# A delta rule's products: VectorE in program order too, copies ahead of SiLUs, sums two chunks at a time, first tiles normed ahead of the weights

## The chip, the cores and the metric

The kernel runs on one core of a Trainium2 chip. The metric is the device time of one execution, in microseconds (us). A core has the engines TensorE (PE; its weight loads are shown apart, as PEld), VectorE (DVE), ScalarE (ACT) and GpSimd (POOL), and SyncE (SP), which here only issues DMAs. Each engine takes its instructions in the order of its own list, and an instruction at the head of a list that waits for another engine holds up all that stand behind it.

## The reference

The kernel computes one block on x, 128 sequences of T = 32 tokens, so 4096 tokens of width 512, in f32: a cross attention, a gated delta rule with its MLP, and a feed-forward part with ternary weights. The part that matters here, with 32 heads of width 16:

```python
h = _rms(x, attn_norm_w)                       # x is layer-normed first
q = silu(silu(_causal_dwconv(h @ Wq.T, conv_q)))   # 4 taps along a sequence
k = silu(silu(_causal_dwconv(h @ Wk.T, conv_k)))
v = silu(silu(_causal_dwconv(h @ Wv.T, conv_v)))
q, k = _l2norm(q by heads), _l2norm(k by heads)
beta = sigmoid(h @ Wbeta.T)
def step(S, (kt, qt, vt, bt)):
    err = S kt - vt
    S = S - bt * outer(err, kt)
    return S, S qt
```

The kernel does not step through the tokens. For each sequence and head it forms the products of all k with all k and all q (32 x 32 each); the k-k products give a triangular system, which is solved by forward substitution for all sequences and heads of a group at once; the q-k products, masked, and the k then give the outputs.

## The kernel before

The program has four stages, one after the other, with some work of a later stage beside an earlier one: the cross attention (0 to about 687 us in the profile), `delta_products` (702 to 1223), `delta_out_mlp` (outputs, MLP and the rest of the substitution, to 2366) and the ternary feed-forward part (to the end). The change lies in the second.

`delta_products` takes the tokens in 8 groups of 512 (NG, SG; GT = 4 tiles of 128 tokens). A group is one round, `a_round`, or `last_round` for the last. A round has 12 steps, one for each 128 channels of k, q and v: k0, q0, k1, q1, ..., then v0 to v3 (the last round goes through k, v, q). Each step does this:

- `channels` (L614): four matmuls of 128x512 into a PSUM tile pp (three buffers); ScalarE copies it into acc, scaled by the last tap (three buffers); VectorE adds the three other taps, each reading and writing acc (L625).
- `activated` (L634): two SiLUs on ScalarE, on the acc of the step before. After a step of q, `masked` calls `hold` (L646), which spreads kq by heads into a zeroed operand kqm (three buffers) with eight DMAs on SP (`masked_operand`, L511).
- `multiply` (L653), in eight of the twelve steps (`due`): `products` (L519), 32 small matmuls pg<-kqm,kq into two PSUM tiles, two ScalarE copies kk<-pg, and on GpSimd the store of the k-k half, the mask and the store of the q-k half.
- `Group.square` and `Group.add`: squares of k and q on ScalarE, and their sums by heads on TensorE, into three column groups of 32 rows of one PSUM tile pn, the middle one being the logits of beta.
- In steps 7 to 10, `normed` (L605): a tile of the next group is normed on VectorE (hn, two buffers), turned by four TensorE transposes and copied to hT by ScalarE.
- `behind_round`, for the group before: `by_tokens` turns lengths and beta to rows of tokens, `put_q` and `put_v` store them and the scaled v, `inverted` inverts the lengths of q (rl).

Beside the rounds from the second on, `mixed` (L106) takes steps of `Substitution.solve` (L471) between the steps of the round, in proportion: `SHARE` units of cost a round, where one solve has 82 units and 8 for the landing of its loads. Its work is on VectorE: for each token s, a scaling of W by a column (L493), a product pr of L with the solved row (L497) and a subtraction from all the rows behind (L503), so the operations get shorter from 128x1984 down to 128x64. Its loads (L in four pieces, W in one) go through SP.

TensorE and ScalarE take the instructions of this stage in program order: `InOrder` (L141) chains each instruction to the one before, and so their rows in the profile all carry L151. VectorE, GpSimd and SP are ordered by a planner, which follows the engines' estimated times and the buffers. Before the first round, `scaled_rows` (L453) multiplies the weights wk, wq, wv and wb by the norm's weights, on VectorE, in 16 slices, and four GpSimd memsets (L1476) clear um and pe, two operands that the third stage uses.

## Time and profile before

| what | value |
|---|---|
| median of three runs | 2940.22 us (2938.33 to 2943.78) |
| the profiled execution's own time | 2938.77 us |
| its span, first to last instruction | 2937.0 us |
| TensorE busy | 2823.2 us, 96% |
| VectorE busy | 1995.4 us, 68% |
| ScalarE busy | 1033.0 us, 35% |
| GpSimd busy | 682.5 us, 23% |
| mean granted clock of TensorE | 0.988 |

In rows of the profile, L12 is line 12 of the kernel. A row of a group names the line, the engine, the operation, output <- inputs by the program's names, and the shape (partitions x elements). A wait is put down to the instruction whose end released it. In a time line, a row has start and duration, and in brackets how long the engine was idle before it, and the releaser; consecutive alike instructions share a row (xN), and their duration is that of the whole row.

### The profile page before, as it was taken

Reading aid. Unit: us, or ns where it says so; the run is one execution under the profiler, and the core shown is the slowest. Engines: PE = TensorE matmul, PEld = TensorE weight load, DVE = VectorE, ACT = ScalarE, POOL = GpSimd, SP = SyncE. Lnnn points to the kernel's source line nnn. Section 1 sums busy time; section 2 is a strip of 40 time slices with the busy share of each in tenths; the row PEclk is TensorE's granted clock in tenths of the full one; section 3 lists DMA queues with packets and bytes.
Section 4 is the critical chain, followed back from the end, with each engine's and each line's share of the span. In section 5 each row is a group of like instructions: output and inputs, shape, how many; then the busy total and the mean of one; then the engine's idle time right before and its main releaser. Section 6 shows DMA issues by size and latency. Waiting matters only on the chain.

```text
span 2937.0 us, 42773 instructions
## 1 busy us (share of the span) xinstructions
PE 2823.2 (96%) x15895; PEld 1658.6 (56%) x15958; DVE 1995.4 (68%) x3317; ACT 1033.0 (35%) x1766; POOL 682.5 (23%) x974
## 2 busy tenths in 40 slices
PE   8999999997999899999999999999999989999997
PEld 3434343443443344566676767777777756666664
DVE  3353544325599995678787878888722289999996
ACT  1111111213666466521122212112211146776774
POOL 1121212212777677321212111101000000000000
PEclk9999999999999999999999999999999999999999
DMA  9898998874555545841414141313231124434433
GB/s 316 275 306 295 337 315 278 280 243 123 149 165 155 163 141 145 242 140 56 130 54 132 56 130 52 122 57 98 71 108 33 35 74 90 87 81 88 89 71 69
DMA packets 342815, 429.64 MB, mean 146 GB/s; under 512 B 149712, under 2 KB 250192, under 8 KB 340176
## 3 DMA queue, kind: packets, MB, share of 16 engines
q1 hardware_dynamic: 305696, 324.36, 37.0%
q0 software_dynamic: 36912, 102.55, 11.7%
q8 instruction: 127, 2.08, 0.3%
q14 instruction: 80, 0.66, 0.1%
HBM read 288.88 MB, written 94.37 MB: 130 GB/s over the span
## 4 chain that ended last, share of the span: by engine, by line
PE 59%; DVE 10%; issue 2%; DMA 2%; POOL 1%; ACT 1%; SPq 1%; ACTq 0%; DVEq 0%; POOLq 0%
PE ps L151 18%; PE pm L1009 9%; PE pm L1020 9%; PE pm L1012 9%; PE pp L151 5%; PE ps L983 4%; DVE W L503 2%; DVE pr L497 2%; DVE acc L625 2%; PE ps L953 2%; PE pg L151 1%; PE pn L151 1%; DMA xs<-x 1%; POOL kk L541 1%; DVE m L151 1%
## 5 line engine op out<-in xcount | busy, mean ns | idle before, releaser
L1009 PE MATMUL pm<-hT,wg 128*128 128x256 f32 x1408 | 343.1, 386 | 0.2 <-ACT hT L998 0.2
L1012 PE MATMUL pm<-hT,wu 128*128 128x256 f32 x1408 | 336.8, 382 | 1.3 <-DVE wu L1070 1.3
L497 DVE TENSOR_TENSOR pr<-L,W 128x1984 f32<-128x1984 f32 (+30 forms) x248 | 307.3, 1239 | 9.1 <-DMA L<-ld 4.6
L503 DVE TENSOR_TENSOR W<-W,pr 128x1984 f32<-128x1984 f32 (+30 forms) x248 | 309.7, 1249 | 2.8
L1020 PE MATMUL pm<-wd,mT 128*128 128x512 f32 x704 | 307.4, 592 | 0.0
L1009 PEld LDWEIGHTS pm<-hT,wg 128*128 128x128 f32 x1408 | 263.9, 191 | 51.0 <-issue 11.5
L1012 PEld LDWEIGHTS pm<-hT,wu 128*128 128x128 f32 x1408 | 268.7, 191 | 38.7 <-DVE wu L1070 1.6
L1020 PEld LDWEIGHTS pm<-wd,mT 128*128 128x128 f32 x704 | 132.4, 190 | 160.2 <-issue 160.2
L151 PE MATMUL ps<-wq,qT 128*128 128x512 bf16 x930 | 215.5, 379 | 6.2 <-ACT t L151 4.6
L1014 ACT ACTIVATE sg<-pm 128x256 f32<-128x256 f32 x176 | 67.4, 383 | 331.4 <-PE pm L1009 319.7
L1015 DVE TENSOR_TENSOR mT<-pm,sg 128x256 f32<-128x256 f32 x176 | 74.0, 420 | 158.7 <-PE pm L1012 155.0
L151 PEld LDWEIGHTS <-qT 128*128 128x128 bf16 x960 | 94.0, 98 | 105.3 <-issue 5.5
L151 DVE TENSOR_TENSOR mb<-m 128x1024 f32<-128x1024 f32 x128 | 153.2, 1217 | 0.1
L151 DVE TENSOR_TENSOR m<-mb 128x1024 f32<-128x1024 f32 x128 | 150.8, 1219 | 1.2
L1343 POOL DMA_DIRECT2D xo<-x x31 | 26.4, 851 | 526.4 <-ACT xo L151 492.0
L151 ACT ACTIVATE t<-ps,magic,qs 128x512 f32<-128x512 f32 x158 | 115.7, 781 | 39.5 <-DVE qs L151 39.4
L537 POOL DMA_DIRECT2D ld<-kk x128 | 93.6, 731 | 147.6 <-ACT kk L151 120.5
L541 POOL TENSOR_TENSOR kk<-kk,cm 128x256 f32<-128x256 f32 x128 | 126.3, 987 | 2.7
L151 PEld LDWEIGHTS ps<-hd,mT 128*128 128x128 f32 x1024 | 119.1, 192 | 8.9 <-ACT mT L151 4.8
L151 PE MATMUL ps<-hd,mT 128*128 128x128 f32 x1024 | 119.8, 275 | 4.0 <-ACT mT L151 4.0
L151 PE MATMUL ps<-wq,q2T 128*128 128x512 bf16 x481 | 116.2, 384 | 5.4 <-DMA q2T<-q 3.7
L151 PE MATMUL pp<-hT,wk 128*128 128x512 f32 x256 | 120.3, 614 | 0.7 <-ACT hT L151 0.7
(224 smaller groups left out, 4751.2 us busy)
## 6 DMA issues: line engine op xcount, KB each, us to landing
kall<-in_ctxT_dram SPq DMA_DIRECT2D x32, 2056.0 KB
cx<-in_ctx_dram SPq DMA_DIRECT2D x32, 2048.0 KB
x<-xo POOLq DMA_DIRECT2D x64, 256.0 KB, 3.5
ld<-kk POOLq DMA_DIRECT2D x128, 128.0 KB, 2.6
pd<-kk POOLq DMA_DIRECT2D x128, 128.0 KB, 2.6
L<-ld SPq DMA_DIRECT2D x32, 512.0 KB
pe<-pd SPq DMA_DIRECT2D x256, 64.0 KB
kqm<-kq SPq DMA_DIRECT2D x448, 32.0 KB
```

The lines of the kernel that those rows point to most:

```text
L151: got = method(*args, **kw)
L497: nc.vector.tensor_mul(pr[:, 0:n], bc(L[:, s, :, s + 1 : T].rearrange("p h t -> p t h"), HD), w[:, s].unsqueeze(1).to_broadcast([P, n, H4, ...
L503: nc.vector.tensor_sub(w[:, s + 1 :], w[:, s + 1 :], pr[:, 0:n])
L537: nc.gpsimd.dma_start(ld[r].rearrange("(i p) f -> p i f", p=P), kk[:, 0].rearrange("p i h t -> p i (h t)"))
L541: nc.gpsimd.tensor_mul(q, q, cm.unsqueeze(1).to_broadcast([P, 2 * H4, T]))
L625: last = nc.vector.scalar_tensor_tensor(acc[:, :, d:], pp[:, :, : T - d], cw[n][:, ec, TAPS - 1 - d : TAPS - d], acc[:, :, d:], ALU.mult, ...
L983: nc.tensor.matmul(pw, oT[:, i, dc, :], wo[:, dc, :], start=dc == 0, stop=dc == DC - 1)
L1009: nc.tensor.matmul(pg, wg[:, dc, fs], hT[:, dc, :], start=dc == 0, stop=dc == DC - 1)
L1012: nc.tensor.matmul(pu, wu[:, dc, fs], hT[:, dc, :], start=dc == 0, stop=dc == DC - 1)
L1014: nc.scalar.activation(sg, pg, AF.Silu)
L1015: mark[:] = [nc.vector.tensor_mul(mT[:, fc, :], pu, sg).ins]
L1020: nc.tensor.matmul(pd, mT[:, fc, i * P : (i + 1) * P], wd[:, fc, :], start=fc == 0, stop=fc == FC - 1,)
```

## The change

VectorE gets an `InOrder` as well, for the products and for the parts of the substitution that run beside them, so it takes its instructions as the program writes them: the three taps of a step one behind the other, then the round's other work, then the pieces of the substitution. In each step `multiply` comes ahead of `activated`. The sums of squares are made for two chunks of channels at once, into four column groups, at two steps of a round instead of four; beta's logits are made apart, at the end of a round, with a transpose of their own; lengths and beta are taken to tokens accordingly. At the start, the first four tiles are normed and turned ahead of the scaling of the weights, and wq is scaled on ScalarE. The norm of a tile (`normed`) now comes one step ahead of its transposes (`turned`). The clearing of um and pe is done by twelve VectorE memsets in the first round, four to a step. The substitution's loads on SP are chained behind the last kqm transfer (`Substitution.load`, `queue`).

```diff
...
 PACE = 45.0
-def scaled_rows(nc, wp, name, norm, ws, engine=None):
-    mul = engine.mul if engine else nc.vector.tensor_scalar_mul
-    nw = wp.tile([P, DC], FP, name=name, bufs=1)
-    nc.sync.dma_start(nw, norm.rearrange("(c p) -> p c", p=P))
-    for t in ws:
-        for dc in range(DC):
-            mul(t[:, dc, :], t[:, dc, :], nw[:, dc : dc + 1])
+def scaled_rows(mul, t, nw):
+    for dc in range(DC):
+        mul(t[:, dc, :], t[:, dc, :], nw[:, dc : dc + 1])
 class Substitution:
...
     def __init__(self, g, pool, ld, vd, ud):
-        self.nc, self.pool, self.ld, self.vd, self.ud = g.nc, pool, ld, vd, ud
+        self.tc, self.nc, self.pool = g.tc, g.nc, pool
+        self.ld, self.vd, self.ud = ld, vd, ud
+        self.dve, self.queue = g.nc.vector, {}
+    def load(self, dst, src):
+        got = self.nc.sync.dma_start(dst, src)
+        if "last" in self.queue:
+            follow(self.tc, got.ins, self.queue["last"])
+            self.queue["last"] = got.ins
     def solve(self, gi):
...
-            nc.vector.tensor_mul(w[:, s], w[:, s], bc(W[:, s, :, HD], HD))
+            self.dve.tensor_mul(w[:, s], w[:, s], bc(W[:, s, :, HD], HD))
...
-                nc.vector.tensor_sub(w[:, s + 1 :], w[:, s + 1 :], pr[:, 0:n])
+                self.dve.tensor_sub(w[:, s + 1 :], w[:, s + 1 :], pr[:, 0:n])
...
     for h in range(HH):
         rows = slice(h * HD, (h + 1) * HD)
-        nc.sync.dma_start(m[rows, h % H4], kq[rows])
+        last = nc.sync.dma_start(m[rows, h % H4], kq[rows])
+    return last.ins
 def products(nc, pe, act, banks, pool, ld, pd, k, m, cm):
...
         )
     )
     pe = InOrder(tc, nc.tensor)
     act = InOrder(tc, nc.scalar)
+    dve = substitution.dve = InOrder(tc, nc.vector)
+    queue = substitution.queue
     with stack:
         w, cw = {}, {}
         for n, src, p in (("k", wkT, wp1), ("v", wvT, wp1), ("q", wqT, wp1)):
...
         nc.sync.dma_start(hs, heads.rearrange("(c p) h -> p c h", p=P))
         cm = wp.tile([P, T], FP, name="cm")
         nc.sync.dma_start(cm, causal)
-        scaled_rows(nc, wp, "nw", norm_w, [w["k"], w["q"], w["v"], w["b"]])
+        nw = wp.tile([P, DC], FP, name="nw")
+        nc.sync.dma_start(nw, norm_w.rearrange("(c p) -> p c", p=P))
         kqm = [wp3.tile([P, H4, 2, KT], FP, name=f"kqm{i}") for i in range(3)]
-        blank = [t[:, h] for t in kqm for h in range(H4)]
+        blank = [t[:, h] for t in kqm for h in range(H4)] + blanks
         mv, rs = stats
         def load(n):
...
             nc.sync.dma_start(xt, x1[n * P : (n + 1) * P, :])
             return xt
-        def normed(n, xt, hT):
+        def normed(n, xt):
+            hn = hp.tile([P, D], FP, name="hn")
+            dve.tensor_scalar(hn, xt, mv[:, n, 0:1], rs[:, n, 1:2], ALU.subtract, ALU.mult)
+            return hn
+        def turned(n, hn, hT):
             i = n % GT
-            hn = hp.tile([P, D], FP, name="hn")
-            nc.vector.tensor_scalar(
-                hn, xt, mv[:, n, 0:1], rs[:, n, 1:2], ALU.subtract, ALU.mult
-            )
             act.copy(hT[:, :, i * P : (i + 1) * P], g.transposed(ps, hn, g.ident, pe=pe))
         def channels(hT, n, ec):
...
             acc = wk.tile([P, GB, T], FP, name="acc", bufs=3)
             act.activation(acc, pp, AF.Copy, scale=cw[n][:, ec, TAPS - 1 : TAPS])
             for d in range(1, TAPS):
-                last = nc.vector.scalar_tensor_tensor(
+                dve.scalar_tensor_tensor(
                     acc[:, :, d:], pp[:, :, : T - d], cw[n][:, ec, TAPS - 1 - d : TAPS - d],
                     acc[:, :, d:], ALU.mult, ALU.add,
                 )
-            return acc.rearrange("p b t -> p (b t)"), last.ins
+            return acc.rearrange("p b t -> p (b t)")
         waiting = []
...
             while len(held) < min(len(pieces), count["done"] + len(kqm)):
                 gi, ec, half, kq = pieces[len(held)]
                 m = kqm[len(held) % len(kqm)]
-                masked_operand(nc, m, kq[:, :, half * KT : (half + 1) * KT])
+                queue["last"] = masked_operand(nc, m, kq[:, :, half * KT : (half + 1) * KT])
                 held.append(m)
         def multiply():
...
             def __init__(self, gi):
                 self.gi = gi
-                self.sums = psn.tile([3 * H, SG], FP, name="pn")
-                self.v = {}
+                self.v, self.sq = {}, []
             def square(self, kq, of="kq"):
                 sq = wk.tile([P, 2, SG], FP, name="sq")
                 ns = slice("kq".index(of[0]), "kq".index(of[-1]) + 1)
                 act.activation(sq[:, ns], kq[:, ns], AF.Square)
-                return sq
-            def add(self, sq, hT, ec, of="kq"):
-                at = dict(start=ec == 0, stop=ec == DC - 1)
+                self.sq.append(sq)
+            def add(self, ec, of="kq"):
+                if ec == 0 and "k" in of:
+                    self.sums = psn.tile([4 * H, SG], FP, name="pn")
+                for n in of:
+                    for r in range(2):
+                        at = (2 * "kq".index(n) + r) * H
+                        last = pe.matmul(
+                            self.sums[at : at + H], hs[:, ec + r, :], self.sq[r][:, "kq".index(n)],
+                            start=ec == 0, stop=ec == DC - 2,
+                        )
+                self.sq.clear()
+                return last
+            def logits(self, hT):
+                pb = ps.tile([P, P], FP, name="ps")
+                for dc in range(DC):
+                    for i in range(GT):
+                        pe.matmul(
+                            pb[i * H : (i + 1) * H], w["b"][:, dc, :], hT[:, dc, i * P : (i + 1) * P],
+                            start=dc == 0, stop=dc == DC - 1,
+                        )
+                self.tanh = st.tile([P, P], FP, name="tanh")
+                act.activation(self.tanh, pb, AF.Tanh, scale=0.5)
+            def lengths(self, of="kq"):
                 if "k" in of:
-                    pe.matmul(self.sums[0:H], hs[:, ec, :], sq[:, 0], **at)
-                    pe.matmul(
-                        self.sums[H : 2 * H], w["b"][:, ec, :], hT[:, ec, :], **at
-                    )
-                if "q" in of:
-                    return pe.matmul(self.sums[2 * H :], hs[:, ec, :], sq[:, 1], **at)
-            def lengths(self, of="kq"):
-                if "k" in of:
-                    f = self.factors = wk.tile([3 * H, SG], FP, name="f", bufs=1)
-                    act.activation(f[H : 2 * H], self.sums[H : 2 * H], AF.Tanh, scale=0.5)
-                for n, r in (("k", slice(0, H)), ("q", slice(2 * H, 3 * H))):
-                    if n in of:
-                        act.activation(self.factors[r], self.sums[r], AF.Sqrt)
+                    self.factors = wk.tile([4 * H, SG], FP, name="f", bufs=1)
+                r = slice("kq".index(of[0]) * 2 * H, ("kq".index(of[-1]) + 1) * 2 * H)
+                act.activation(self.factors[r], self.sums[r], AF.Sqrt)
             def by_tokens(self):
                 f = self.factors
-                pt = ps.tile([P, GT, 2 * H], FP, name="ps")
+                pt = ps.tile([P, GT + 2, 2, H], FP, name="ps")
                 for i in range(GT):
                     pe.transpose(
-                        pt[:, i, :], f[0 : 2 * H, i * P : (i + 1) * P], g.ident[0 : 2 * H, 0 : 2 * H]
+                        pt[:, i].rearrange("p r h -> p (r h)"), f[0 : 2 * H, i * P : (i + 1) * P],
+                        g.ident[0 : 2 * H, 0 : 2 * H],
                     )
+                pe.transpose(pt[:, GT:].rearrange("p i r h -> p (i r h)"), self.tanh, g.ident)
                 self.n = st.tile([P, GT, H], FP, name="n")
-                nc.vector.tensor_scalar_max(self.n, pt[:, :, 0:H], 1e-12)
+                for r in range(2):
+                    to, of = (
+                        t.rearrange("p i (c r h) -> p i c r h", c=2, r=2)[:, :, :, r]
+                        for t in (self.n, pt[:, 0:GT, r])
+                    )
+                    dve.tensor_scalar_max(to, of, 1e-12)
                 self.beta = st.tile([P, GT, H], FP, name="beta")
-                nc.vector.tensor_scalar(self.beta, pt[:, :, H:], 0.5, 0.5, ALU.mult, ALU.add)
+                dve.tensor_scalar(
+                    self.beta.rearrange("p i h -> p (i h)"),
+                    pt[:, GT:].rearrange("p i r h -> p (i r h)"), 0.5, 0.5, ALU.mult, ALU.add,
+                )
                 n2 = st.tile([P, GT, H], FP, name="n2", bufs=1)
...
             def put_q(self):
                 for c in range(DC):
-                    rows = slice(2 * H + c * HH, 2 * H + (c + 1) * HH)
+                    at = (2 + c % 2) * H + c * HH
+                    rows = slice(at, at + HH)
...
-                nc.vector.tensor_mul(
+                dve.tensor_mul(
                     vt[:, :, :, 0:HD], pv.rearrange("p i (h v) -> p i h v", v=HD),
                     bc(self.n[:, :, h], HD),
                 )
...
-                acc, last = channels(hT, n, ec)
-                with tc.issue_after(last):
-                    for _ in range(min(H4, len(blank))):
-                        nc.vector.memset(blank.pop(0), 0.0)
+                acc = channels(hT, n, ec)
+                for _ in range(min(H4, len(blank))):
+                    dve.memset(blank.pop(0), 0.0)
+                if due[j] and count["done"] < len(held) and (old or j >= 4):
+                    multiply()
                 activated()
                 waiting.append((acc, dst, masked(ec) if n == "q" else kept))
-                if due[j] and count["done"] < len(held) and (old or j >= 4):
-                    multiply()
                 if 3 <= j <= 9 and j % 2:
-                    sq = new.square(kq[(j - 3) // 2])
-                if 4 <= j <= 10 and j % 2 == 0:
-                    new.add(sq, hT, (j - 4) // 2)
+                    new.square(kq[(j - 3) // 2])
+                if j in (6, 10):
+                    new.add((j - 6) // 2)
                 if j in loads:
                     xt.append(load((gi + 1) * GT + len(xt)))
                 if j == 9 and gi == 0:
                     g.factors(*(t[:, EARLY:] for t in stats))
                 if j == 11:
+                    new.logits(hT)
                     new.lengths()
                 if 7 <= j <= 10:
-                    normed((gi + 1) * GT + j - 7, xt[j - 7], hT_next)
+                    turned((gi + 1) * GT + j - 7, hn, hT_next)
+                if 6 <= j <= 9:
+                    hn = normed((gi + 1) * GT + j - 6, xt[j - 6])
                 behind_round(old, j)
                 yield 1
...
+                if count["done"] < len(held):
+                    multiply()
                 activated()
                 waiting.append((acc, dst, stored(ec) if n == "q" else kept))
-                if count["done"] < len(held):
-                    multiply()
-                if 3 <= j <= 6:
-                    new.add(sq, hT, j - 3, "k")
+                if j in (4, 6):
+                    new.add(j - 4, "k")
                 if 2 <= j <= 5:
-                    sq = new.square(kq[j - 2], "k")
+                    new.square(kq[j - 2], "k")
                 if j == 7:
+                    new.logits(hT)
                     new.lengths("k")
                 if j == 8:
                     new.by_tokens()
...
-                if j == 11:
-                    new.add(sq, hT, 0, "q")
                 if j >= 10:
-                    sq = new.square(kq[j - 10], "q")
+                    new.square(kq[j - 10], "q")
                 behind_round(old, j)
                 yield 1
             activated()
-            for ec in range(1, DC):
-                if ec > 1:
-                    sq = new.square(kq[ec], "q")
-                sums = new.add(sq, hT, ec, "q").ins
-                if ec > 1:
-                    left["pe"].append(sums)
+            new.add(0, "q")
+            for ec in (2, 3):
+                new.square(kq[ec], "q")
+            left["pe"].append(new.add(2, "q").ins)
             new.lengths("q")
             left["act"].append(act.last)
             new.put_q()
         hT = wk1.tile([P, DC, SG], FP, name="hT")
         for i in range(GT):
-            normed(i, load(i), hT)
+            turned(i, normed(i, load(i)), hT)
+        for n, mul in (
+            ("k", dve.tensor_scalar_mul), ("b", dve.tensor_scalar_mul), ("q", act.mul),
+            ("v", dve.tensor_scalar_mul),
+        ):
+            scaled_rows(mul, w[n], nw)
         old = None
         for gi in range(NG - 1):
             made = []
             mixed((len(todo), a_round(gi, old, hT, made)), *beside(gi))
             old, hT = made
         mixed((len(todo), last_round(NG - 1, old, hT)), *beside(NG - 1))
-        assert count["done"] == len(pieces)
+        assert count["done"] == len(pieces) and not blank
+    substitution.dve = nc.vector
+    queue.clear()
     return left
...
-        for t in (*um, *pe):
-            nc.gpsimd.memset(t, 0.0)
...
+            [t[:, :, e] for t in um for e in range(2)] + [t[:, c, 2 * j : 2 * j + 2] for t in pe for c in range(2) for j in range(2)],
...
```

More of the change, by code (lines that the diff above doesn't have):

```diff
@@ L477, in load @@
         def load(s):
-            nc.sync.dma_start(
-                L[:, s : s + some].rearrange("p s h t -> p s (h t)"), rows[:, s : s + some]
-            )
+            self.load(L[:, s : s + some].rearrange("p s h t -> p s (h t)"), rows[:, s : s + some])
         load(0)
         W = self.pool.tile([P, T, H4, HD + 1], FP, name="W", bufs=2)
-        nc.sync.dma_start(
+        self.load(
             W.rearrange("p t h v -> p (t h v)"),
@@ L496, in solve @@
                 pr = self.pool.tile([P, T - 1, H4, HD], FP, name="pr")
-                nc.vector.tensor_mul(
+                self.dve.tensor_mul(
                     pr[:, 0:n],
@@ L545, in products, with inverted @@
         )
-def inverted(nc, rq, r):
+def inverted(nc, dve, rq, r):
     every = rq.rearrange("i h c t -> (i h c) t")
@@ L553, in inverted @@
     yield
-    nc.vector.tensor_scalar_max(r, r, 1e-12)
-    nc.vector.reciprocal(r, r)
+    dve.tensor_scalar_max(r, r, 1e-12)
+    dve.reciprocal(r, r)
     nc.gpsimd.dma_start(every, r)
@@ L561, in delta_products @@
     g: Ctx, x1, stats, norm_w, wqT, wkT, wvT, conv_q, conv_k, conv_v, wbT, heads, causal, ld, vd,
-    pd, rq, kd, beside,
+    pd, rq, kd, beside, substitution, blanks,
 ):
@@ L676, in square @@
                 act.activation(sq[:, ns], kq[:, ns], AF.Square)
-                return sq
-            def add(self, sq, hT, ec, of="kq"):
-                at = dict(start=ec == 0, stop=ec == DC - 1)
-                if "k" in of:
-                    pe.matmul(self.sums[0:H], hs[:, ec, :], sq[:, 0], **at)
-                    pe.matmul(
-                        self.sums[H : 2 * H], w["b"][:, ec, :], hT[:, ec, :], **at
-                    )
-                if "q" in of:
-                    return pe.matmul(self.sums[2 * H :], hs[:, ec, :], sq[:, 1], **at)
+                self.sq.append(sq)
@@ L707, in by_tokens @@
                 self.beta = st.tile([P, GT, H], FP, name="beta")
-                nc.vector.tensor_scalar(self.beta, pt[:, :, H:], 0.5, 0.5, ALU.mult, ALU.add)
+                dve.tensor_scalar(
+                    self.beta.rearrange("p i h -> p (i h)"),
+                    pt[:, GT:].rearrange("p i r h -> p (i r h)"), 0.5, 0.5, ALU.mult, ALU.add,
+                )
                 n2 = st.tile([P, GT, H], FP, name="n2", bufs=1)
-                nc.vector.tensor_mul(n2, self.n, self.n)
-                nc.vector.reciprocal(n2, n2)
@@ L712, in by_tokens @@
-                nc.vector.tensor_mul(self.beta, self.beta, n2)
+                dve.tensor_mul(n2, self.n, self.n)
+                dve.reciprocal(n2, n2)
+                dve.tensor_mul(self.beta, self.beta, n2)
             def put_q(self):
                 for c in range(DC):
-                    rows = slice(2 * H + c * HH, 2 * H + (c + 1) * HH)
+                    at = (2 + c % 2) * H + c * HH
+                    rows = slice(at, at + HH)
                     nc.gpsimd.dma_start(
@@ L729, in put_v @@
                 h = slice(ec * HH, (ec + 1) * HH)
-                nc.vector.tensor_mul(
+                dve.tensor_mul(
                     vt[:, :, :, 0:HD], pv.rearrange("p i (h v) -> p i h v", v=HD),
@@ L752, in behind_round @@
                 old.inverse = inverted(
-                    nc, rq[old.gi], st.tile([P, P], FP, name="rl", bufs=1)
+                    nc, dve, rq[old.gi], st.tile([P, P], FP, name="rl", bufs=1)
                 )
@@ L828, in last_round @@
                 before = len(nc.cur_bb.bb.instructions)
-                acc, _ = channels(hT, n, ec)
+                acc = channels(hT, n, ec)
                 if (n, ec) == ("q", DC - 2):
@@ L1116, in inverse @@
             r = lp.tile([P, 2, 2, H4, T], FP, name="kk").rearrange("p n i h t -> p (n i h t)")
-            for _ in inverted(nc, rq[NG - 1], r[:, 0:P]):
+            for _ in inverted(nc, nc.vector, rq[NG - 1], r[:, 0:P]):
                 yield 1
@@ L1501, in perceiver_block @@
             g, x1, stats, attn_norm_w, wqT, wkT, wvT, conv_q, conv_k, conv_v, wbT,
-            heads, causal, ld, vd, pd, rq, kd, beside_products,
+            heads, causal, ld, vd, pd, rq, kd, beside_products, substitution,
+            [t[:, :, e] for t in um for e in range(2)] + [t[:, c, 2 * j : 2 * j + 2] for t in pe for c in range(2) for j in range(2)],
         )
```

## The prediction

> **What bounds the kernel now.** I read the page first, then engine time by stretch, the waits of TensorE, and the time line where a stretch was longer than its neighbours. From the page, the 40 slices and the chain of work that ended last:
>
> ```profile
> PE   8999999997999899999999999999999989999997
> DVE  3353544325599995678787878888722289999996
> PE 59%; DVE 10%; issue 2%; DMA 2%; POOL 1%; ACT 1%; SPq 1%; ACTq 0%; DVEq 0%; POOLq 0%
> ```
>
> TensorE is full nearly everywhere, but VectorE holds 10% of the chain, and it is full in slices 12 to 15, about 810 to 1100 us: the products of the delta rule, the stage that is changed. I cut that stage at the first product of each of its eight rounds. Columns: stretch, length, busy time (and count) of PE, PEld, DVE, ACT, POOL, then granted clock, DMA share, GB/s:
>
> ```profile
> 702.10:760.80 58.70, 57.31 (x329) 23.89 (x329) 31.41 (x50) 32.02 (x53) 21.83 (x30) 0.97 0.33 87
> 760.80:821.30 60.50, 59.60 (x421) 25.81 (x413) 40.04 (x55) 39.57 (x65) 41.99 (x62) 1.00 0.60 173
> 821.30:885.90 64.60, 61.06 (x416) 26.17 (x412) 64.50 (x78) 40.36 (x65) 54.29 (x66) 1.00 0.56 155
> 885.90:951.90 66.00, 61.97 (x417) 26.57 (x413) 65.62 (x94) 40.45 (x66) 49.34 (x66) 0.97 0.56 156
> 951.90:1030.10 78.20, 65.94 (x417) 27.63 (x413) 72.05 (x98) 40.64 (x65) 55.12 (x67) 0.89 0.55 166
> 1030.10:1094.60 64.50, 60.85 (x417) 25.86 (x413) 61.89 (x83) 40.18 (x66) 49.78 (x66) 1.00 0.48 132
> 1094.60:1154.50 59.90, 59.80 (x417) 25.85 (x413) 33.36 (x52) 40.07 (x67) 47.37 (x70) 1.00 0.53 145
> 1154.50:1222.60 68.10, 67.34 (x373) 30.20 (x368) 41.88 (x71) 48.04 (x75) 37.04 (x62) 1.00 0.75 202
> ```
>
> Call them rounds 0 to 7; they add to 520.5 us. Round 6 has little substitution beside it and no wait: 59.9. In rounds 2 and 3 VectorE is busy all of 130.6 us; round 4 is the worst. The waits of TensorE from 660 to 1230 us (total, times, longest):
>
> ```profile
> PE pg L151 <- ACT kk L151: 16.2, 13, 2.6
> PE ps L151 <- DVE hn L609: 11.4, 1, 11.4
> PE pg L151 <- DMA kqm<-kq: 9.8, 3, 7.7
> ```
>
> The first is a chain: TensorE waits for ScalarE's copy out of PSUM (kk), which stands behind a SiLU, which waits for VectorE's taps. TensorE's and ScalarE's time lines at 948 us show it (start, duration, ..., idle before and its releaser):
>
> ```profile
> 950.33 1.62 PE L151 MATMUL pg<-kqm,kq 64*32 64x256 f32 x32 [1.65 <-ACT kk L151]
> 951.88 5.29 PE L151 MATMUL pp<-hT,wk 128*128 128x512 f32 x8
> ```
> ```profile
> 948.51 0.63 ACT L151 ACTIVATE acc<-acc 128x512 f32<-128x512 f32 x1 [4.27 <-DVE acc L625]
> 949.17 0.63 ACT L151 ACTIVATE v<-acc 128x512 f32<-128x512 f32 x1
> 949.71 1.05 ACT L151 COPY kk<-pg 128x512 f32<-128x512 f32 x2
> ```
>
> The wait of 1.65 us is only half its price: the next product takes 5.29 us where 3.6 is usual (the same shape at 957.00), with a mean clock of 0.89 over that round. The second wait is the start of the stage:
>
> ```profile
> 688.92 3.80 DVE L460 TENSOR_SCALAR wk<-wk,nw 128x512 f32<-128x512 f32 x1
> 698.86 0.99 DVE L609 TENSOR_SCALAR hn<-xt,mv,rs 128x512 f32<-128x512 f32 x2
> 699.54 1.94 PE L151 MATMUL ps<-ident,hn 128*128 128x128 f32 x8 [11.39 <-DVE hn L609]
> ```
>
> VectorE scales 16 weight slices before it norms the third and fourth tile of the first round (the first two were normed and turned by 688); the wk slice beside GpSimd's memsets takes 3.80 us, a quiet one 0.41.
>
> **The start.** After, VectorE does xo (ends 688.0), bn (0.69), the two norms (0.55 each) and the aggregate (0.16): the last hn by about 690. Transposes (0.5 per four) and ScalarE's copies (0.59 each) end near 691.4. Four wk slices at 0.41 are done by then too, as the memsets are no longer beside them; ScalarE takes wq (four at about 0.6), wanted only a step (3.6 us) later. First product about 692 instead of 702.15: **-10 us**. The twelve or so memsets of half a microsecond (a 128x512 one takes 0.49) go onto VectorE in round 0, 5.8 us where it is busy 31 of 59: nothing, and if that cover were gone, 5.8. GpSimd loses its four memsets, 5.7 us that no product waited for, and put_q keeps its number of transfers: nothing. The first loads go out on SP ahead of the scaling, where SP has nothing else: nothing.
>
> **TensorE's work in a round.** Round 6, 59.9, less two product groups that ran slow there (1.80 and 1.52 against 1.09, together 1.1): 58.7. Four additions of three sums each (0.99) become two of four (taken at 0.99 each, since column groups ran beside one another): -2.0. The beta logits come out as 32 narrow instructions; the nearest row, the 128*32 matmuls of the next stage, gives 1.50 us for 44, so 1.1; one more transpose, 0.11. TensorE alone: 57.9 us. Bounds for the logits: 0.6 (hidden in other columns) and 2.0 (as before).
>
> **VectorE's work in a round, in order.** The three taps of a step depend on each other and are now consecutive. VectorE's own time line has both cases:
>
> ```profile
> 842.41 0.69 DVE L625 SCALAR_TENSOR_TENSOR acc<-pp,cwk,acc 128x464 f32<-128x464 f32 x1
> 1112.89 2.21 DVE L625 SCALAR_TENSOR_TENSOR acc<-pp,cwq,acc 128x496 f32<-128x496 f32 x3
> ```
>
> A tap beside other work occupies 0.63 from start to start (the next operation starts at 843.02); three in a row 2.21, or 2.14 from start to start. So 12 x 2.14 = 25.7, with norms 2.2, vt 2.4, the lengths' chain 2.3 and rl 1.2 (durations of the same rows): 33.8. The substitution: its pr and W groups take 307.3 and 309.7 over eight solves, 77.1 a solve, less about 5 of overlap plus 9 for the small scalings: 81. A round gets 24.3 of the 82 cost units of one solve: 24.0. Together 57.8. The rows of rounds 2 and 3 add to about 126 of 130.6 us with VectorE always busy, so x 1.035: 59.8. That is above TensorE's 57.9. I take 60.5 for rounds 2, 3, 4 and 6, leaving 0.7 for the joints; 59.5 for round 5, which has a landing pause in its share; 59 for round 1 (half a share); 57 for round 0; and 68.5 for round 7, where VectorE has about 66 and TensorE 64 to 65. Ends: 57.9 (TensorE alone) and 64 (as slow as round 2 or 5 before).
>
> The Trainium skill, "VectorE: DVE Perf Modes", section "The DRAIN you can't avoid", says that every operation pays its own pipe flush and that leaving out semaphores between operations saves nothing. By it taps in a row would cost no more than interleaved ones, 12 x 1.89 = 22.6, and TensorE would pace at 57.9; the rows above disagree (2.14 against 1.89), and the sum goes by them.
>
> **Copies ahead of SiLUs.** ScalarE's order becomes copies (1.05), then SiLUs. The copies need only TensorE's own groups, so 16.2 us of waits go, and the slow products behind them. What is late instead: the SiLU starts 1.05 later, and so does a masked operand, whose eight transfers take some 5 us of SP, three steps ahead of use; covered, or at most 1 us a step. This saving is inside the round times above, not beside them. The 7.7 us wait for kqm in round 4 came from one W load of 8.3 us at 977 ahead of the kqm transfers; after, loads stand behind the last masked operand, yet two sets of loads still precede one first kqm, in rounds 5 and 6. I take 1 of 7.7 as still paid, inside the 0.7.
>
> **The new wait.** VectorE in order stops at whatever is not ready. The norm of the fourth tile waits for a load that stands on SP behind a set of kqm transfers; taps are queued behind it, then SiLUs, then products. About 2 us of stall, covered by three PSUM buffers (two steps, 7 us). Price below: rival C.
>
> The Trainium skill, "TensorE: Matmul & The Clock Gate", section "What's actually happening", has the clock halve only after an idle window of about 3.4 us. By it the short waits would cost only themselves, and their removal saves 16, not 16 and more; the row of 5.29 us after a wait of 1.65 disagrees here, and speaks against any new short waits that the order brings.
>
> **Sum.** 57 + 59 + 4 x 60.5 + 59.5 + 68.5 = 486, against 520.5: -34.4. With the start: -44.4. The profiled execution took 2938.8 us (span 2937.0); it becomes 2894.4. The median shown, 2940.2, is 1.5 above the profiled one: **2896 us**.
>
> **Rivals.** *B, TensorE paces.* If the taps overlap better than the row, rounds cost 56, 6 x 57.9, 65: 468.4, 52 less, and 2878. For it: round 6 at 59.8 busy of 59.9. Against: the sum of VectorE's rows. *A, VectorE paces worse.* Taps wait for their predecessor and for ScalarE, pieces fill no gaps: 64 a full round, 58 + 60 + 4 x 64 + 61 + 72 = 507; 2917. For it: 32 waits of VectorE for acc in the trace; against: the fixed order removes some. *D, the copies' waits stay* in another place (the fix doesn't act), start alone: 2930. *C, slower.* VectorE stands at the fourth norm behind a late load, with taps behind it, and TensorE idles long enough to clock down. It decides from 44 / 7 = 6.3 us a round; at 8 us (a stall of 4.5 beyond the cover and 3.5 of slow products, twice the pair above) 56 are lost: 2952. For it: such loads stand behind up to two kqm sets, 10 us of SP; against: three PSUM buffers.
>
> **Chances.** Main 0.51 (its own range 2886 to 2906), B 0.17, A 0.18, D 0.05, C 0.09. The range runs from B to beyond A, 2876 to 2923, leaving out D and C and the tails. No change means within 0.2%, 5.9 us, about what a measurement of this kernel can tell. Faster: main, A, B and most of D, 0.88; same 0.03; slower 0.09.
>
> **What the changed profile would show.** First product near 692; the waits for kk gone from TensorE's list; taps in groups of three at 2.2; full rounds near 60.5 with VectorE 95% busy and clock 1.00 in round 4; the two later stages unchanged in length. I am wrong if VectorE shows waits for xt or hn with taps behind them, if TensorE waits for DVE taps through pp, or if the later stages move by more than 3 us.

## The result, and the profile after

The changed kernel takes 2951.36 us (median, 2949.49 to 2955.28), against 2941.22 us for the kernel before beside it: a ratio of 1.0043, 95% interval 1.0031 to 1.0054. Forecast was 2896, faster; it is slower, by some 10 us. VectorE's rows in the products carry L151 now too, as it is in hand order.

The profiled executions differ by 14.2 us (spans 2951.2 and 2937.0). Four marks divide this: the last xo of the first stage (687.31 before, 691.05 after), the first product of round 0 (702.15, 695.19), the first gate product of the MLP (1230.02, 1242.99), and the end. The first stage, which the change doesn't touch, ends 3.7 us later; the start of the products is 10.7 shorter; the eight rounds and the way into the MLP are 19.9 longer; the rest is 1.2 longer. So the start came as forecast, and the rounds lost where 34 us were to be won.

Engine time by stretch, cut as before at the first product of each round (the last stretch, which reaches to the MLP's first gate product, is 75.6 us in the kernel before):

```profile
695.20:758.20 63.00, 56.89 (x352) 24.77 (x352) 40.30 (x71) 35.84 (x58) 21.79 (x30) 0.95 0.34 96
758.20:830.00 71.80, 62.37 (x442) 28.16 (x437) 36.16 (x55) 40.04 (x65) 44.47 (x65) 0.93 0.52 152
830.00:894.10 64.10, 61.01 (x441) 26.91 (x437) 59.28 (x71) 39.96 (x65) 50.72 (x65) 0.97 0.50 134
894.10:960.30 66.20, 60.91 (x441) 27.20 (x437) 59.75 (x73) 40.03 (x65) 47.38 (x65) 0.97 0.54 150
960.30:1025.30 65.00, 60.95 (x444) 27.22 (x438) 59.44 (x88) 40.13 (x65) 49.49 (x66) 0.97 0.49 134
1025.30:1096.00 70.70, 61.83 (x441) 27.55 (x437) 55.16 (x80) 40.12 (x65) 48.62 (x66) 0.95 0.62 176
1096.00:1161.90 65.90, 60.79 (x441) 27.20 (x437) 57.34 (x71) 39.95 (x65) 50.26 (x65) 0.97 0.52 147
1161.90:1243.00 81.10, 71.01 (x421) 33.49 (x417) 73.17 (x109) 50.40 (x82) 45.12 (x67) 0.96 0.68 191
```

Round 1, with little of the substitution beside it, lost most, 11.3 us; rounds 0, 5 and 6 and the last stretch lost 4.4, 6.2, 6.0 and 5.5, and only round 4 won much, 13.3. VectorE can't be the pace in round 1: it is busy 36 of 72 us there. The waits of TensorE, 660 to 1240 us:

```profile
PE ps L151 <- DVE hn L151: 16.3, 8, 4.1
PE pg L151 <- DMA kqm<-kq: 12.0, 10, 2.5
PE ps L151 <- DVE W L151: 11.8, 2, 7.5
```

The waits for the copies kk are gone from the list. In their place TensorE waits for hn (the two put down to W are the same wait: W is the operation behind hn on VectorE, 0.46 us later). VectorE's own waits, and its time line in round 1:

```profile
DVE hn L151 <- DMA xt<-x: 35.6, 7, 9.7
```
```profile
809.13 2.22 DVE L151 SCALAR_TENSOR_TENSOR acc<-pp,cwv,acc 128x496 f32<-128x496 f32 x3 [2.02 <-ACT acc L151]
821.07 0.55 DVE L151 TENSOR_SCALAR hn<-xt,mv,rs 128x512 f32<-128x512 f32 x1 [9.72 <-DMA xt<-x]
...
823.93 2.21 DVE L151 SCALAR_TENSOR_TENSOR acc<-pp,cwv,acc 128x496 f32<-128x496 f32 x3
```

Once a round, seven times, VectorE stands at the norm of a tile that isn't loaded, with taps behind it. SP's time line in round 2 says why the load is late, and TensorE's what it costs:

```profile
845.67 37.05 SPq L519 DMA_DIRECT2D kqm<-kq  x56
882.82 0.53 SPq L609 DMA_DIRECT2D xt<-x  x1
```
```profile
883.36 1.07 PE L151 MATMUL pn<-sq,hs 128*32 128x512 f32 x8
886.40 0.63 PE L151 MATMUL ps<-ident,hn 128*128 128x128 f32 x4 [1.97 <-DVE hn L151]
886.86 5.30 PE L151 MATMUL pp<-hT,wv 128*128 128x512 f32 x8
```

SP issues seven sets of eight kqm transfers in a row, 0.66 us each, 37 us, and only then the load of the fourth tile. The load's buffer, one of three, had been free for 15 us: the tile before in it was normed from 866.86 to 867.87. Seven sets stand ahead of it in each of the seven rounds that load tiles (with loads of L and W among them in rounds 1 and 5); the norm is due earlier. After each of the seven longest waits (1.97 to 7.50 us) the next product takes 4.65 to 5.53 us where 3.60 is usual.

The kernel before has the same loads and the same slow SP. There the planner norms tiles well ahead: in its time line two norms stand at 700.67 and 702.24, directly behind those of the first four tiles, as round 0 begins; they are the second group's. Tiles normed early free their buffers early, so SP could issue the loads ahead of a round's kqm transfers. This is its time line at the head of round 1:

```profile
761.69 4.29 SPq L602 DMA_DIRECT2D xt<-x  x4
774.90 27.51 SPq L516 DMA_DIRECT2D kqm<-kq  x40
```

The third of these four loads, at 762.82, is for the tile that the changed kernel loads at 818.03. Hand order put each norm one step ahead of its transposes and gave up this lead.

### The profile page after: what moved, and what is told of

It reads as the page before. It is cut to its first block, busy times and chain, and to the rows that moved or that the text cites. A ratio compares the mean times of both kernels' runs of the same rounds, so it can differ in the third digit from the quotient of the medians.

```text
span 2951.2 us, 43234 instructions
## 1 busy us (share of the span) xinstructions
PE 2831.1 (96%) x16158; PEld 1671.0 (57%) x16158; DVE 2011.1 (68%) x3333; ACT 1034.4 (35%) x1763; POOL 673.0 (23%) x970
## 4 chain that ended last, share of the span: by engine, by line
PE 78%; DVE 10%; DMA 5%; issue 3%; SPq 3%; ACT 1%; POOL 0%; DVEq 0%; ACTq 0%; POOLq 0%
PE ps L151 19%; PE pm L1050 9%; PE pm L1053 9%; PE pm L1061 8%; PE ps L395 8%; PE pp L151 7%; PE ps L1024 3%; PE ps L293 3%; PE ps L360 3%; PE ps L346 3%; SPq L519 2%; PE ps L313 2%; DVE W L506 2%; PE ps L994 2%; PE ps L97 2%
## 5 line engine op out<-in xcount | busy, mean ns | idle before, releaser
L1050 PEld LDWEIGHTS pm<-hT,wg 128*128 128x128 f32 x1408 | 263.5, 191 | 50.8 <-issue 11.4
L1053 PEld LDWEIGHTS pm<-hT,wu 128*128 128x128 f32 x1408 | 268.7, 191 | 38.6 <-DVE wu L1111 1.6
L500 DVE TENSOR_TENSOR pr<-L,W 128x832 f32<-128x832 f32 (+30 forms) x199 | 238.0, 1196 | 7.7 <-DMA L<-ld 3.8
L506 DVE TENSOR_TENSOR W<-W,pr 128x832 f32<-128x832 f32 (+30 forms) x199 | 238.1, 1197 | 2.4
L151 PE MATMUL ps<-wq,qT 128*128 128x512 bf16 x960 | 217.1, 379 | 3.0 <-ACT t L151 3.0
L1055 ACT ACTIVATE sg<-pm 128x256 f32<-128x256 f32 x176 | 67.2, 383 | 330.0 <-PE pm L1050 322.9
L1056 DVE TENSOR_TENSOR mT<-pm,sg 128x256 f32<-128x256 f32 x176 | 73.7, 419 | 155.6 <-PE pm L1053 152.4
L151 DVE TENSOR_TENSOR mb<-m 128x1024 f32<-128x1024 f32 x128 | 153.2, 1217 | 0.1
L151 PEld LDWEIGHTS <-qT 128*128 128x128 bf16 x960 | 94.0, 98 | 103.7 <-issue 3.9
L151 DVE TENSOR_TENSOR m<-mb 128x1024 f32<-128x1024 f32 x128 | 150.8, 1219 | 1.2
L151 ACT ACTIVATE t<-ps,magic,qs 128x512 f32<-128x512 f32 x158 | 115.7, 781 | 37.8 <-DVE qs L151 37.8
L151 PEld LDWEIGHTS ps<-hd,mT 128*128 128x128 f32 x1024 | 122.4, 196 | 9.4 <-ACT mT L151 5.3
L151 PE MATMUL ps<-hd,mT 128*128 128x128 f32 x1024 | 123.1, 280 | 4.6 <-ACT mT L151 4.6
L151 PE MATMUL pp<-hT,wv 128*128 128x512 f32 x256 | 125.8, 638 | 0.0
L151 PE MATMUL ps<-wq,q2T 128*128 128x512 bf16 x512 | 119.8, 389 | 2.6 <-DMA q2T<-q 2.6
L293 PE MATMUL ps<-wv,hT 128*128 128x512 f32 x256 | 120.9, 616 | 0.0
```

Of the source, the lines that this page charges most:

```text
L151: got = method(*args, **kw)
L293: nc.tensor.matmul(pv, hT[:, dc, i * P : (i + 1) * P], w["v"][:, dc, :], start=dc == 0, stop=dc == DC - 1,)
L500: self.dve.tensor_mul(pr[:, 0:n], bc(L[:, s, :, s + 1 : T].rearrange("p h t -> p t h"), HD), w[:, s].unsqueeze(1).to_broadcast([P, n, H4, ...
L506: self.dve.tensor_sub(w[:, s + 1 :], w[:, s + 1 :], pr[:, 0:n])
L1050: nc.tensor.matmul(pg, wg[:, dc, fs], hT[:, dc, :], start=dc == 0, stop=dc == DC - 1)
L1053: nc.tensor.matmul(pu, wu[:, dc, fs], hT[:, dc, :], start=dc == 0, stop=dc == DC - 1)
```

## The experiments

Times are medians; each ratio is to the kernel before, run beside it (2937.8 to 2942.0 us).

**The load ahead.** The changed kernel, with the fourth load one step earlier, at the head of its step, and ahead of the sixth kqm set: the next kqm transfer on SP is chained behind it.

```diff
-        loads = (2, 3, 4, 8)
+        loads = (2, 3, 4, 7)
...
+        if after:
+            follow(tc, last.ins, after.pop())
```

> The changed kernel with one edit: the load of a round's fourth tile is issued on SP one step earlier and ahead of the sixth set of kqm transfers, where in the changed kernel it stands behind the seventh set, which itself waits for step 8's products. Theory N (VectorE in order stands at the norm of the fourth tile, waiting for that load, with taps queued behind it): the waits of TensorE for hn and for the operation behind it (16.3 + 11.8 us) go, and with them the slow products behind them (5.3 to 5.5 us instead of 3.6, about six of them, 11 us): about 39 us less, near 2912. Rival P (VectorE's work paces the rounds, the stall only shows where): VectorE is busy 59.3 to 59.8 of 64 to 66 us in the full rounds already, rounds come down to 62 or 63 at most, about 15 less, near 2936. If the load lands late all the same: 2951.

2918.66 us, ratio 0.9922 (0.9905 to 0.9938): 33 us below the changed kernel, where theory N had 39. Theory N holds, and rival P falls. The waits for hn are gone but for 0.2 us; rounds 0 to 5, by stretch:

```profile
690.20:747.40 57.20, 54.54 (x352) 23.65 (x352) 40.16 (x71) 35.77 (x58) 21.80 (x30) 1.00 0.33 90
747.40:807.40 60.00, 58.44 (x441) 26.24 (x437) 35.92 (x54) 39.81 (x65) 44.82 (x64) 1.00 0.57 167
807.40:870.30 62.90, 60.73 (x441) 27.28 (x437) 59.09 (x71) 39.85 (x65) 52.53 (x66) 0.97 0.56 154
870.30:931.70 61.40, 59.25 (x441) 26.34 (x437) 59.12 (x74) 39.94 (x65) 47.87 (x65) 1.00 0.55 152
931.70:992.60 60.90, 59.34 (x442) 26.39 (x438) 58.82 (x88) 40.02 (x65) 49.29 (x65) 1.00 0.55 151
992.60:1059.70 67.10, 60.88 (x441) 27.25 (x438) 54.97 (x79) 39.99 (x65) 48.14 (x67) 0.95 0.61 179
```

With round 6 (62.6 us) and the last round and the way into the MLP (81.3) they add to 513.4 us: 34.4 less than in the changed kernel, which I take as the price of the stall, and 14.5 less than before. Outside these stretches the two executions differ too, by 5.0 us less in the first stage and 6.6 us more from the MLP on, which the edit does not touch. What TensorE still waits for in the rounds is kqm:

```profile
PE pg L151 <- DMA kqm<-kq: 15.0, 11, 3.4
```

**The load on another queue.** The changed kernel, with that load issued by GpSimd, nothing else moved:

```diff
-        def load(n):
+        def load(n, by=nc.sync):
...
-            nc.sync.dma_start(xt, x1[n * P : (n + 1) * P, :])
+            by.dma_start(xt, x1[n * P : (n + 1) * P, :])
...
-                    xt.append(load((gi + 1) * GT + len(xt)))
+                    xt.append(load((gi + 1) * GT + len(xt), nc.gpsimd if j == 8 else nc.sync))
```

> The changed kernel with one edit: the load of a round's fourth tile is issued by GpSimd instead of SP, in the same step. Theory S (SP is the late one: it issues seven sets of eight kqm transfers at about 0.65 us each, 37 us in a row, ahead of that load, in each round): the load comes as soon as its buffer is free, TensorE's waits for hn go, 2915 to 2925 as with the load ahead on SP. Rival (the load is late because its buffer comes free late): 2945 to 2952.

2912.04 us, ratio 0.9907 (0.9885 to 0.9928), 3 us below theory S's range. Of TensorE's waits for hn this is left:

```profile
PE ps L151 <- DVE hn L151: 0.9, 2, 0.7
```

The wait was SP's backlog, not the buffer: theory S holds. Another queue for seven loads is worth 39 us.

**VectorE back to the planner,** all else as changed:

```diff
-    dve = substitution.dve = InOrder(tc, nc.vector)
+    dve = substitution.dve = nc.vector
```

> The changed kernel with VectorE left to the planner, as in the kernel before; all other parts of the change stay. Theory N: the planner norms tiles ahead of their round, so the stall at the fourth tile goes; start (-10) and the copies ahead of the SiLUs (-16 of waits) stay: near 2910. Rival: the copies ahead of the SiLUs and the sums bring nothing while the taps are interleaved with the substitution: only the start remains, 2930. If the stall comes from the fourth load's place whatever orders VectorE: 2945 or more.

2927.02 us, ratio 0.9955 (0.9939 to 0.9971): the seven stalls go, as N has it (one wait for hn, 4.1 us, is left), but the rest brings 17 us less than forecast, near the rival's 2930. The rest of the change is worth little more than its start. Hand order is not bad in itself: with the load on GpSimd it is ahead of this run, and the two intervals do not overlap (0.9885 to 0.9928 against 0.9939 to 0.9971). Whether the planner's order would gain from that load too was not tried.

**VectorE in order alone,** on the kernel before (`nc.vector` becomes the InOrder in the products and the substitution beside them):

```diff
     act = InOrder(tc, nc.scalar)
+    dve = substitution.dve = InOrder(tc, nc.vector)
...
-            nc.vector.tensor_scalar(
+            dve.tensor_scalar(
```

> The kernel before with one edit: VectorE in program order in the products and in the substitution beside them. Theory N: the norm of a tile now stands right ahead of its own transposes and behind a load that is late, so TensorE stalls in each of seven rounds, 4 to 8 us each and a slow product behind it, and the waits for the copies kk remain or grow: 2960 to 2990. Rival (the order itself costs nothing, the norm's place one step earlier does): 2935 to 2945.

3036.73 us, ratio 1.0310 (1.0288 to 1.0333): worse than I had it, and in another way:

```profile
PE ps L151 <- DVE hn L151: 82.7, 26, 11.4
```

One of these, the 11.4 us, is the start's, as before; with three that are put down to W (10.7 us in all), 28 are left, one for each of four tiles in seven rounds, of some 3 us each. A tile's norm is written right ahead of its transposes, so on VectorE it comes behind the taps of its own step, and TensorE waits for both. The changed kernel norms a step earlier; there, waits for hn beyond 0.3 us are left only for the tile whose load is late.

**The start alone,** on the kernel before (norms and transposes ahead of the scaling, wq on ScalarE):

```diff
-        scaled_rows(nc, wp, "nw", norm_w, [w["k"], w["q"], w["v"], w["b"]])
...
+        dve = InOrder(tc, nc.vector)
         for i in range(GT):
-            normed(i, load(i), hT)
+            normed(i, load(i), hT, dve)
+        for n, mul in (
+            ("k", dve.tensor_scalar_mul), ("b", dve.tensor_scalar_mul), ("q", act.mul),
+            ("v", dve.tensor_scalar_mul),
+        ):
+            scaled_rows(mul, w[n], nw)
```

> The kernel before with the start of the change alone: the first four tiles normed and turned ahead of the scaling of the weights, wq scaled on ScalarE; GpSimd's memsets stay. If the start's time goes through to the end, as the sum had it: 10 to 11 us less, near 2931. Rival: the first round waits for something else (masked operands, or scaling beside the memsets) and gives it back: 2938 to 2942.

2934.74 us, ratio 0.9968 (0.9955 to 0.9982): 7 us less by the medians, 9 by the ratio. From the last xo of the first stage to the first product it is 8.2 us, where the kernel before had 14.8 and the changed kernel 4.1: 6.7 us less, and not 10 to 11, as GpSimd's memsets stay and one of the norms beside them takes 4.07 us. The start's gain, as large as it is here, goes through to the end.

**The copies ahead of the SiLUs alone,** on the kernel before (and the same in the last round):

```diff
+                if due[j] and count["done"] < len(held) and (old or j >= 4):
+                    multiply()
                 activated()
                 waiting.append((acc, dst, masked(ec) if n == "q" else kept))
-                if due[j] and count["done"] < len(held) and (old or j >= 4):
-                    multiply()
```

> The kernel before with one edit: the products and their copies ahead of the SiLUs in each step. If the waits for kk (16.2 us in all, with slow products behind the longer ones) come from the SiLUs ahead of the copies, they go: 16 to 25 us less, 2916 to 2925. Rival: TensorE then waits for the taps through pp or for the masked operands instead, and nothing is won: 2936 to 2943.

2944.95 us, ratio 1.0009 (0.9997 to 1.0021): nothing. The waits were moved:

```profile
PE pg L151 <- DMA kqm<-kq: 14.1, 9, 2.4
...
PE pp L151 <- DVE acc L625: 7.2, 6, 2.9
PE pn L151 <- ACT sq L151: 3.1, 4, 1.2
PE ps L151 <- ACT f L151: 3.1, 1, 3.1
```

These are 27.5 us, against 26.0 for kk and kqm before; none for kk is left.

**The SiLUs first again,** with the load ahead and VectorE in order (and the same in the last round):

```diff
-                if due[j] and count["done"] < len(held) and (old or j >= 4):
-                    multiply()
                 activated()
                 waiting.append((acc, dst, masked(ec) if n == "q" else kept))
+                if due[j] and count["done"] < len(held) and (old or j >= 4):
+                    multiply()
```

> The changed kernel with the load ahead (as in the run of the load ahead), and the SiLUs ahead of the products and copies again, in every step. Theory K (the copies ahead of the SiLUs delay the masked operand, and TensorE waits for kqm instead of kk; the waits are moved, not removed): the 15.0 us of waits for kqm go, waits for kk of about the same size come, 2912 to 2925. Rival (the copies ahead are a gain once VectorE is in order): 16 to 25 us slower, 2935 to 2944.

2918.65 us, ratio 0.9903 (0.9881 to 0.9925), level with the load ahead. In hand order no wait of TensorE for kk returns, perhaps because the taps are not held up by long substitution pieces; that reason was not tested. The copies' place brings nothing there either. Waits for kqm fall to 5.9 us, and waits for hn and W (10.7 us) take their place.

**The SiLU first in step 2 alone,** with the load ahead:

```diff
+                if j == 2:
+                    activated()
                 if due[j] and count["done"] < len(held) and (old or j >= 4):
                     multiply()
```

> The changed kernel with the load ahead, and with the SiLUs ahead of the products in step 2 alone, the step that releases a round's first masked operands. Theory K (full rounds are 60 to 62 us because the first masked operands of a round come 0.6 to 1.5 us late, not because VectorE paces): waits for kqm fall from 15.0 to 7 or less, rounds 1 to 4 and 6 come down by 1 to 2 us each, 2908 to 2912. Rival P (VectorE's 59 us of work paces the full rounds): waits move, the time stays at 2918.

2912.19 us, ratio 0.9892 (0.9870 to 0.9914). Waits for kqm fall from 15.0 to 6.5 us, and the time is in the range of theory K, though its interval overlaps that of the load ahead. Rounds 1 to 4 and 6 change by -0.7, -1.6, -0.6, +1.3 and -3.0.

**Both mends,** the load on GpSimd and the SiLU first in step 2 (the two diffs above, on the changed kernel):

> The changed kernel with both mends: the fourth load issued by GpSimd, and the SiLUs ahead of the products in step 2 alone. If the two causes are separate (the late load, 7 x 5 us, and the late first masked operands, about 6 us in all): 2904 to 2909, with waits for kqm of 7 us or less and none over 2 us for hn. Rival (one hides the other: with the load early, the masked operands are covered otherwise): 2911 to 2914, as each mend gave by itself on top of an early load.

2915.89 us, ratio 0.9925 (0.9904 to 0.9946), beyond the rival's range too and no better than either. Waits for kqm are 6.0 us, those for hn and W 7.9, the longest 2.4. Whether the second mend is worth anything isn't settled; the first is.

**No substitution beside the last round,** with the load ahead:

```diff
-            return [(SHARE, part(all_u, SHARE))] if gi else []
+            return [(SHARE, part(all_u, SHARE))] if 0 < gi < NG - 1 else []
```

> The changed kernel with the load ahead, and no pieces of the substitution beside the last round (they are done beside the MLP instead). Theory L (the last round and the way into the MLP, 81.3 us against 75.6 before, are longer because VectorE, in order, does its full share there, 73 us busy where the planner's order had 46): they come down to 75 or 76 and the time to 2912 to 2914. Rival: the MLP takes it back, or the way into it is long for another reason: 2917 to 2920.

2947.56 us, ratio 1.0011 (0.9998 to 1.0023). Half of theory L holds: the last round and the way into the MLP shrink from 81.3 to 73.7 us. But from there to the end it is 1744.5 us instead of 1714.8, four times the gain taken back, as TensorE waits there for solved values:

```profile
PE ps L1002 <- POOL um L984: 23.6, 5, 6.6
```

**The substitution's loads on GpSimd,** on top of the SiLU first in step 2:

```diff
-        got = self.nc.sync.dma_start(dst, src)
-        if "last" in self.queue:
-            follow(self.tc, got.ins, self.queue["last"])
-            self.queue["last"] = got.ins
+        (self.nc.gpsimd if "last" in self.queue else self.nc.sync).dma_start(dst, src)
```

> The run with the load ahead and the SiLU first in step 2, with one edit more: the substitution's loads beside the products are issued by GpSimd, not chained behind the kqm transfers on SP. If SP's order is what makes round 5 long (64.8 us against 59.6 to 62.2 of the other full rounds: the loads of L and W stand ahead of its first masked operands): round 5 comes to 61 and the time to about 2908. Rival (the transfers themselves, 1088 KB for W, delay the masked operands wherever they are issued): no change, 2912; GpSimd, 50 us busy of 60, may also be late with its stores: up to 2920.

2922.55 us, ratio 0.9939 (0.9921 to 0.9957): slower, a little beyond what the rival allowed. Round 5 is 68.1 us instead of 64.8, and round 1 64.9 instead of 59.3, so taking these loads off SP does not shorten it. Whether it is the 1088 KB of W or GpSimd's own lateness stays open.

**The sums alone,** on the kernel before (`add`, `logits`, `lengths`, `by_tokens` and `put_q` as in the change, its other parts undone):

```diff
-                if 4 <= j <= 10 and j % 2 == 0:
-                    new.add(sq, hT, (j - 4) // 2)
+                if j in (6, 10):
+                    new.add((j - 6) // 2)
...
                 if j == 11:
+                    new.logits(hT)
                     new.lengths()
```

> The kernel before with the sums of the change alone: two chunks at once into four column groups, the logits of beta apart. From the trace of the changed kernel, sums of a round take 2 x 1.07 + 1.08 + 0.17 = 3.4 us where they took 4 x 0.99 = 4.0: 0.6 us a round, 4 to 5 us in all at most, 2936 to 2942. Rival: the rounds that VectorE paces don't see it and ScalarE's tanh and longer root add to the round's end: 2942 to 2948.

2944.46 us, ratio 1.0010 (0.9998 to 1.0022): nothing, or a loss too small to tell. I take it that 0.6 us of TensorE's work a round don't show where waits set the round; no run tests that. Not tried alone were the memsets on VectorE and the chaining of the substitution's loads.

## Why the prediction was wrong

**The step that failed** is the new wait: "About 2 us of stall, covered by three PSUM buffers (two steps, 7 us)". Both halves were wrong. The load does not stand behind one set of transfers, or the two that rival C allowed, but behind seven in a row, 37 us of SP's issuing, and VectorE stood 2.8 to 9.7 us. And PSUM buffers are no cover for it: they let TensorE run ahead of the taps, but the transposes of that very tile stand in TensorE's own order in the next step. TensorE waits for the norm itself, 28.1 us in all, with slow products behind it. That was rival C, given 9 in 100; its place and mechanism were right, its price of 8 us a round was too high: 34.4 us over seven rounds, 4.9 each. At that rate alone it would not have turned the sign, by the bound of 6.3; the other misses did that.

**The start** was right: -10 forecast, -10.7 in the trace, -7 to -9 when done alone, with GpSimd's memsets still beside it.

**The rounds without the stall** were forecast at 57, 59, 60.5, 60.5, 60.5, 59.5 and 60.5; with the load ahead they are 57.2, 60.0, 62.9, 61.4, 60.8, 67.2 and 62.6. VectorE's work was sized well (59.8 us forecast, 59 measured in full rounds), though the spacing of 0.63 us read for a tap beside other work is 0.61 in the row shown and 0.63 only over the three taps. But VectorE does not pace, as the main forecast had it: rounds 1 and 4 are 60.0 and 60.8 with VectorE at 36 and 59. From round 1 on TensorE itself is busy 58.4 to 60.9 us of a round, slow products included, where 57.9 was forecast, so rival B (TensorE paces) is nearer to these rounds than the main forecast. The one wait of size left is kqm; with the SiLU first in step 2 it more than halved, and rounds 1 to 4 and 6 moved by only -3.0 to +1.3 us each. Round 5 is the largest miss, 7.7 us: TensorE waits 2.8 and 3.4 us for its first masked operands, with L and W loaded ahead of them; "1 of 7.7 as still paid" was mis-sized. Why it is so long stays open, as issuing those loads from GpSimd did not shorten it.

**The last round** was put at 0.4 us more than before, and it is 5.5 more to the MLP (5.7 with the load ahead). With the planner VectorE was busy 46 of 75.6 us there; in order it does its full share, 73 of 81. Without that share the stretch was 73.7.

**The copies ahead of the SiLUs** were to take off the 16.2 us. They took off the row of that name and nothing of the time. "Covered, or at most 1 us a step" was wrong for the masked operand: a SiLU behind the products comes later, and eight transfers at 0.66 us follow it before TensorE can go on.

**The sum of the misses**: 34.4 for the stall, and 20.0 between the forecast and the rounds with the load ahead (7.7 in round 5, 5.3 in the last, 7.0 in the others), 54.4 together: the forecast of -34.4 becomes the +20 measured. The later stages stayed within 3 us, as said.

The Trainium skill, "TensorE: Matmul & The Clock Gate", section "What's actually happening", has the clock fall after an idle window of some 3.4 us. In these runs shorter waits were followed by slow products too, but not always: one of 1.97 us by a product of 5.30 us (changed kernel), one of 1.33 us by 5.29 (the load ahead, at 1088.94), yet one of 1.45 us by 3.70 (changed kernel, round 0) and one of 1.86 us by 3.60 (the SiLU first in step 2, at 919.02). So a wait below 2 us can cost more than itself here, and its length alone does not tell whether it will.

## What to carry to other kernels

Before fixing an engine's order by hand, list what the planner did ahead of time for it, here norms up to two tiles early and the loads that this lets go out early, and check for each waiting instruction whether its data can be there at its new place, by counting what the issuing queue must send first. An engine that issues transfers is a resource like any other: 64 small ones at 0.66 us fill 42 of a round's 60 us, and the order on that queue decides. A wait that disappears from a list has not been saved until the time says so: the copies ahead of the SiLUs moved their waits and won nothing.

## What was not expected of the hardware

The transfers' issue, not their bytes, sets the pace of SP: 56 of 32 KB took 37.05 us in a row in round 2, and 37.8 to 38.6 in the other rounds that have no load of L or W among them; the issue of one takes 0.59 us, that of a load of 256 KB 0.53. In round 1 SP also stood 2.7 us for the landing of W ahead of kqm transfers, which do not read W. In the trace the transfer that stood waits for the semaphore by which the load of W tells of its landing, and then uses it for its own; so the reuse of semaphores is the likely reason, but no run tried it.
